# Layer 0's second product as seven block products in a hand-written order, with the weight sums and the transfers around it rearranged

## The chip, the cores and the metric

One core of one Trainium2 chip. The metric is device time in microseconds (us) of one execution. The kernel before takes 1918.76 us, the median of 3 runs (1918.51 to 1919.03). All runs told of here are of the fast state, at a mean granted TensorE clock of 0.995 to 1.00. "Ratio" is always the mean time of one kernel's fast runs over the mean time of the fast runs of the kernel before in the same rounds, with its 95% interval. It is therefore not quite the ratio of the medians quoted beside it.

## The reference, cut to what matters

Four layers run one after the other on x of 128 x 64 x 256 in f32: a graph network, an LSTM over sliding windows, causal attention, and masked attention. Only layer 0's second product, the start of layer 1 and one round of layer 3 are touched.

```python
# layer 0, after the aggregation over neighbours; rows = 8192 (16 chunks of 512)
h   = relu(batchnorm(agg @ W1.T + b1))     # 512 features
out = h @ W2.T + b2                        # 512 -> 256: the product that is changed
out = batchnorm(out)                       # needs mean and variance over all rows
x   = x + out
# layer 1 begins with a graph aggregation; then, for p = 1..4, an LSTM over windows:
g = x_t @ Wih[p].T + h @ Whh[p].T + (bih + bhh)
```

## The kernel before: the parts that count

The second product of one chunk has an output of 256 features x 512 rows, in two blocks of 128 features. Each block sums four matmuls of 512 columns.

```python
def product2(chunks, by_block):
    h1 = {c: l0b.tile([P, KH, CH], F32, tag="h1") for c in chunks}
    banks = {(c, m): bank(f"z2_{c}_{m}") for c in chunks for m in range(KD)}
    for k in range(KH):
        for c in chunks:                                   # batch norm and ReLU, ScalarE
            nc.scalar.activation(h1[c][:, k, :], z1[c][k], AF.Relu, bias=..., scale=...)
    for c, m, k in order:                                  # 8 matmuls of 512 columns
        nc.tensor.matmul(banks[c, m], w2_sb[:, k, m*P:(m+1)*P], h1[c][:, k, :], ...)
    for c in chunks:
        for m in range(KD):                                # VectorE: statistics, then eviction
            nc.vector.bn_stats(st2[:, m, c, :], banks[c, m])
            nc.vector.tensor_scalar(z2[c][:, m, :], banks[c, m], bn2_sb[...], None, op0=OP.add)
```

Beside it GpSimd prepares the LSTM's weights for a seven-product scheme of its own. Twelve gates go, one after the other, through two buffers: load, four sums, store.

```python
def weight_sums(p, q):
    w = stage.tile([P, 16, P], F32, tag="ws", bufs=2)
    nc.sync.dma_start(w[...], wih_t / whh_t)               # two loads
    for dst, a, b, op in (...):                            # four sums on GpSimd
        nc.gpsimd.tensor_tensor(v[:, :, dst], v[:, :, a], v[:, :, b], op)
    nc.sync.dma_start(far[:, :9], w[:, :9])                # two stores
    nc.sync.dma_start(far[:, 9:], w[:, 10:])

for c in range(2, NCH):
    if wanted: weight_sums(*wanted.pop(0))
    product2([c], False)
...
bias = ...; nc.sync.dma_start(bias, bih); nc.sync.dma_start(bias2, bhh)
nc.vector.tensor_add(bias, bias, bias2)                    # the LSTM's bias
...
load_sets(6)                                               # prepared weights, six gates
... early <- x                                             # x of the first chunks
```

## Time and profile before

| What | Before |
|---|---|
| Median time | 1918.76 us |
| Span of the profiled execution | 1916.9 us |
| TensorE busy | 1896.7 us (99%) |
| Second product, all 16 chunks, from its first matmul to the one after it | 143.90 to 255.08 us: 111.18 us |
| One chunk in it | 16 records x 0.429 = 6.87 us |
| GpSimd's last weight sums stored | issued at 216.4 us, 39 us before the end of the stretch |
| x issued, x used | 243.25 us, 261.06 us |

How to read it: TensorE is busy in all but 20 us, so a gain comes from fewer columns streamed through it. The other engines matter only where they hold it up. The lines behind this are shown in the prediction. One more row serves for the comparison later: a stretch of 6.05 us in the middle of the product in the kernel before. Columns: PE, PEld (weight loads), DVE (VectorE), ACT (ScalarE) and POOL (GpSimd) busy, each with its number of instructions, then granted clock, DMA share and GB/s.

```profile
186.80:192.85 6.05, 6.05 (x16) 2.68 (x15) 2.03 (x4) 2.11 (x4) 4.73 (x7) 1.00 0.51 202
```

VectorE and ScalarE are a third busy; GpSimd runs ahead with the weight sums at its own pace.

### The profile page before, as it was taken

What the parts mean: (1) busy time and instruction counts of PE and PEld (TensorE: products, weight loads), DVE (VectorE), ACT (ScalarE), POOL (GpSimd) and SP (SyncE); (2) the same over time, 40 slices, a digit from 0 to 9 for tenths busy, and PEclk for the clock granted to TensorE, in tenths of its full rate; (3) what the DMA queues carried; (4) which work ended last, traced back from release to release, by engine and by line L of the source; (5) the groups of instructions that cost most, each with busy time, mean ns of one, the idle gap of its engine ahead of it and who ended that gap; (6) DMA issues with size and microseconds to landing.
All of it is one profiled execution on the core that took longest, in us unless ns stands there. A gap on an engine that the chain in (4) does not pass through costs nothing.

```text
span 1916.9 us, 38323 instructions
## 1 busy us (share of the span) xinstructions
PE 1896.7 (99%) x14981; PEld 1459.5 (76%) x14981; DVE 1158.1 (60%) x3020; ACT 957.9 (50%) x2132; POOL 414.0 (22%) x615
## 2 busy tenths in 40 slices
PE   9999999999999999999999999999999999999998
PEld 5444465897897889699689789879969967777776
DVE  6644354546557655755755765665555557777776
ACT  5654434445456455455545645545554534444453
POOL 4205210221211121121121121112112113232232
PEclk9999999999999999999999999999999999999999
DMA  4216712224524521532542452253144245444433
GB/s 138 67 32 228 275 49 67 83 83 160 159 83 144 181 100 61 177 105 94 187 143 83 160 182 84 72 196 109 59 160 127 92 128 159 133 143 146 143 111 111
DMA packets 110500, 240.36 MB, mean 125 GB/s; under 512 B 11376, under 2 KB 74352, under 8 KB 110320
## 3 DMA queue, kind: packets, MB, share of 16 engines
q1 hardware_dynamic: 109568, 236.57, 37.1%
q8 instruction: 119, 1.95, 0.4%
q0 software_dynamic: 320, 1.05, 0.2%
q14 instruction: 61, 0.50, 0.1%
q10 hardware_dynamic: 432, 0.30, 0.1%
HBM read 169.98 MB, written 67.90 MB: 124 GB/s over the span
## 4 chain that ended last, share of the span: by engine, by line
PE 94%; DVE 3%; ACT 1%; issue 1%; POOL 1%; DMA 0%; DVEq 0%; SPq 0%; ACTq 0%; POOLq 0%
PE x L848 23%; PE g L812 18%; PE z L848 11%; PE y L848 6%; PE z L377 6%; PE v L1120 6%; PE z L360 5%; PE p_q L1127 3%; PE u L593 3%; PE v L579 3%; PE X L1316 3%; PE Y L1316 1%; PE agg_c L214 1%; PE o L1241 1%; PE agg_b L214 1%; PE o L1443 1%
## 5 line engine op out<-in xcount | busy, mean ns | idle before, releaser
L857 DVE TENSOR_TENSOR gates<-gates,x 128x128 f32<-128x128 f32 (+2 forms) x384 | 119.4, 322 | 335.6 <-PE x L848 333.4
L848 PE MATMUL x<-xd,wset 128*128 128x128 f32 (+2 forms) x1280 | 284.9, 310 | 0.1
L848 PE MATMUL x<-hd,wset 128*128 128x128 f32 (+2 forms) x1152 | 246.7, 303 | 0.0
L848 PEld LDWEIGHTS x<-xd,wset 128*128 128x128 f32 x1280 | 202.1, 190 | 16.9 <-DVE gates L857 3.0
L906 POOL TENSOR_TENSOR gates<-gates 128x512 f32<-128x512 f32 (+2 forms) x48 | 74.8, 1559 | 648.1 <-ACT gates L740 648.1
L740 ACT ACTIVATE gates<-gates,bias 128x256 f32<-128x256 f32 (+4 forms) x384 | 170.4, 491 | 66.4 <-DVE gates L857 63.6
L848 PEld LDWEIGHTS x<-hd,wset 128*128 128x128 f32 x1152 | 185.1, 191 | 5.0
L791 ACT ACTIVATE gates<-g,bias 128x512 f32<-128x512 f32 (+2 forms) x240 | 138.0, 609 | 98.1 <-PE g L812 94.8
L812 PE MATMUL g<-hT,wset 128*128 128x256 f32 (+2 forms) x744 | 184.4, 405 | 1.1 <-DVE hT L751 1.1
L812 PEld LDWEIGHTS g<-hT,wset 128*128 128x128 f32 x744 | 140.5, 190 | 44.1 <-issue 8.9
L812 PE MATMUL g<-hT,wih 128*128 128x512 f32 x384 | 166.4, 592 | 0.0
L854 ACT COPY gates<-y 128x128 f32<-128x128 f32 (+2 forms) x192 | 54.1, 293 | 205.2 <-PE y L848 204.7
L848 PE MATMUL z<-hs,wset 128*128 128x128 f32 (+2 forms) x768 | 154.1, 303 | 0.0
L812 PEld LDWEIGHTS g<-hT,wih 128*128 128x128 f32 x384 | 72.3, 190 | 87.7 <-issue 83.2
L848 PEld LDWEIGHTS z<-hs,wset 128*128 128x128 f32 x768 | 119.8, 191 | 3.3
L360 PE MATMUL z<-agg,w_sb 128*128 128x512 f32 x256 | 114.1, 598 | 0.0
L797 DVE TENSOR_TENSOR cell<-gates 128x512 f32<-128x512 f32 (+2 forms) x80 | 50.5, 648 | 100.3 <-ACT gates L791 100.3
L377 PE MATMUL z<-h,w_sb 128*128 128x512 f32 x256 | 110.2, 592 | 0.0
L857 DVE TENSOR_TENSOR gates<-gates,z 128x128 f32<-128x128 f32 (+2 forms) x384 | 104.6, 316 | 0.1
L854 ACT COPY gates<-x 128x128 f32<-128x128 f32 (+2 forms) x192 | 56.5, 295 | 93.9 <-PE x L848 93.1
L740 ACT ACTIVATE gates<-x,bias 128x128 f32<-128x128 f32 (+2 forms) x192 | 74.7, 389 | 50.9 <-PE x L848 48.1
L848 PE MATMUL z<-hT,wset 128*128 128x128 f32 (+1 forms) x512 | 96.9, 301 | 0.0
(245 smaller groups left out, 3637.1 us busy)
## 6 DMA issues: line engine op xcount, KB each, us to landing
wset<-wfar SPq DMA_DIRECT2D x96, 960.0 KB, 6.4
hT<-far_h SPq DMA_DIRECT2D x124, 128.0 KB, 2.8
far_h<-hm SPq DMA_DIRECT2D x16, 512.0 KB, 4.1
far_n<-xs SPq DMA_DIRECT2D x16, 512.0 KB, 6.6
xs<-far_n SPq DMA_DIRECT2D x64, 128.0 KB, 3.4
far_x<-xs SPq DMA_DIRECT2D x16, 512.0 KB, 3.0
x<-far_x SPq DMA_DIRECT2D x64, 128.0 KB, 3.2
xt<-in_x_dram SPq DMA_DIRECT2D x15, 512.0 KB, 4.0
```

The lines of the kernel that those rows point to most:

```text
L360: nc.tensor.matmul(ps, w1_sb[:, k, m * P : (m + 1) * P], agg[:, k, :], start=(k == 0), stop=(k == KD - 1))
L377: nc.tensor.matmul(banks[c, m], w2_sb[:, k, m * P : (m + 1) * P], h1[c][:, k, :], start=(k == 0), stop=(k == KH - 1))
L579: nc.tensor.matmul(banks[m], wg0_sb[:, k, m * P : (m + 1) * P], agg[:, k, :], start=(k == 0), stop=(k == KD - 1))
L740: nc.scalar.activation(gate(q, c, part), src, AF.Tanh if q == 2 else AF.Sigmoid, bias=bs[:, q * KD + c : q * KD + c + 1])
L791: nc.scalar.activation(columns_of(gate(q, c)), natural(banks[q, c][:, :n].rearrange("p (w b) -> p w b", b=nb)), AF.Tanh if q == 2 else AF. ...
L812: nc.tensor.matmul(banks[q, c][:, :n].rearrange("p (w b) -> p w b", b=nb)[:, w, :], block(q, c, k), hv[:, k, w.start * p : (w.stop - 1) * ...
L848: nc.tensor.matmul(folded(self.psum(kind)), wsets[p, self.q][:, BLOCKS[kind][i], :], (ox[self.s] if part == "x" else oh)[kind], start=firs ...
L854: nc.scalar.copy(gate(self.q, kind // 5, halves[kind // 5]), self.psum(kind))
L857: nc.vector.tensor_add(gate(self.q, *dst), gate(self.q, *a), self.psum(kind))
L906: nc.gpsimd.tensor_mul(gates[:, 0, :, :n], gates[:, 0, :, :n], gates[:, 2, :, :n])
L1120: nc.tensor.matmul(ps[:, i, :], hT[:, k, j, :], w[:, k, first : first + D], start=(k == 0), stop=(k == KD - 1))
L1316: nc.tensor.matmul(st[c, tag][:, i * CH // 2 : (i + 1) * CH // 2].rearrange("p (a n) -> p a n", n=P), w, st[c, "o7"][kind], start=first an ...
```

## The change

The output of a chunk is cut into 2 x 2 blocks (features x rows), and the eight block products become seven by forming sums of the weight's blocks once and four sums of the chunk's blocks each time (the Strassen-Winograd form). This is done for chunks 2 to 14; chunks 0, 1 and 15 stay as they were. The scheduler that the kernel is built with no longer orders VectorE, ScalarE and GpSimd in this part: they are put in order by hand, as TensorE was before. The weight sums now stand behind the chunk's own sum in GpSimd's order. x is transferred ahead of the six weight sets, and one round of layer 3 has an exponential behind a copy instead of ahead of it.

The diff, cut to its core (conditions for the first and last chunks left out; `...` marks what is cut):

```diff
+    def differences(engine, dst, b11, b12, b21, b22, third=None):
+        t1, t2, t3, t4 = dst
+        return [lambda: engine.tensor_tensor(t1, b12, b11, OP.subtract),
+                lambda: ((third or engine).tensor_tensor(t3, b22, b12, OP.subtract),
+                         engine.tensor_tensor(t2, b22, t1, OP.subtract)),
+                lambda: engine.tensor_tensor(t4, b21, t2, OP.subtract)]
...
+        for dst, u, v, op in (...):                       # once: sums of w2's blocks
+            nc.gpsimd.tensor_tensor(w2_sums[:, dst], u, v, op)
...
-        for c in range(2, NCH):
-            if wanted:
-                weight_sums(*wanted.pop(0))
-            product2([c], False)
+        for c in range(2, NCH - 1):                       # a = chunk c, b = c + 1, z = c - 1
+            weights = weight_sums(*wanted.pop(0)) if wanted else None
+            next(weights)                                 # loads
+            a.product(2, "Z")
+            if c == 2:
+                ... a.sums ...; result2(0, m, banks[0, m])
+            b.relu(0)
+            z.product(7, "X");  z.add(1, 1, "X")          # frees bank X for product 4
+            b.relu(1)
+            a.product(1, "X");  a.copy(0, 0, "X")
+            z.stats(0)
+            a.product(5, "Y");  a.copy(1, 1, "Y")
+            b.relu(2)
+            a.add(0, 0, "Z")
+            if c == 2: result2(1, m, banks[1, m])
+            z.product(4, "X");  z.copy(1, 0, "X")
+            b.relu(3);  b.begin();  b.sums[0]()
+            z.stats(1)
+            a.product(6, "X");  a.copy(0, 1, "X")
+            b.sums[1]()
+            next(weights)                                 # GpSimd's four sums, stores
+            a.product(3, "Y");  a.add(0, 1, "Y")
+            b.sums[2]()
+            if c in (3, 4):
+                for m in range(KD): stats2(c - 3, m)      # statistics of chunks 0 and 1
...
-    load_sets(6)                                          # the six weight sets
...
+            if n == 1:                                    # now behind the first use of x
+                load_sets(6)
...
-        for c in range(SUP + 2, NCH - SUP - 1):
+        run(ROUND.replace("exp3-3 q2+0 copyq2+0", "q2+0 copyq2+0 exp3-3"), SUP + 2)
+        for c in range(SUP + 3, NCH - SUP - 1):
             run(ROUND, c)
```

More of the change, by code (lines that the diff above doesn't have):

```diff
@@ L324 @@
     st1 = w0.tile([P, KH, NCH, 6], F32, name="st1")
-    z1, hs, aggs = {}, {}, {}
+    z1, z1whole, h1, hs, aggs = {}, {}, {}, {}, {}
     def load0(c):
@@ L356, in product1 @@
                 aggregate0(1)
-                ln_apply(hs[2], *stats2, "a2")
+                ln_apply(hs[2], *third, "a2")
             ps = bank(f"z1_{c}_{m}")
@@ L363, in product1, with relu2 @@
             nc.vector.bn_stats(st1[:, m, c, :], z1[c][m])
-        z2[c] = lo
+        z2[c], z1whole[c] = lo, (lo, hi)
+    def relu2(c, k):
+        nc.scalar.activation(h1[c][:, k, :], z1[c][k], AF.Relu, bias=sh1[:, k : k + 1],
+                             scale=sc1[:, k : k + 1])
     def product2(chunks, by_block):
-        h1 = {c: l0b.tile([P, KH, CH], F32, tag="h1", name=f"h1_{c}") for c in chunks}
         banks = {(c, m): bank(f"z2_{c}_{m}") for c in chunks for m in range(KD)}
-        for k in range(KH):
-            for c in chunks:
-                nc.scalar.activation(h1[c][:, k, :], z1[c][k], AF.Relu, bias=sh1[:, k : k + 1],
-                                     scale=sc1[:, k : k + 1])
         order = [(c, m, k) for c in chunks for m in range(KD) for k in range(KH)]
@@ L378, in product2, with result2, stats2 @@
                              start=(k == 0), stop=(k == KH - 1))
-        for c in chunks:
-            for m in range(KD):
-                nc.vector.bn_stats(st2[:, m, c, :], banks[c, m])
-                nc.vector.tensor_scalar(z2[c][:, m, :], banks[c, m], bn2_sb[:, 0, m : m + 1], None,
-                                        op0=OP.add)
+        return banks
+    def result2(c, m, ps):
+        nc.vector.tensor_scalar(z2[c][:, m, :], ps, bn2_sb[:, 0, m : m + 1], None, op0=OP.add)
+    def stats2(c, m):
+        nc.vector.bn_stats(st2[:, m, c, :], z2[c][:, m, :])
@@ new lines, in new_h1, with __init__, relu, begin @@
+    def new_h1(c):
+        h1[c] = l0b.tile([P, KH, CH], F32, tag="h1", name=f"h1_{c}")
+    class Seven2:
+        def __init__(self, c):
+            self.c, self.banks = c, {}
+            self.b = {(k, j): a[:, :, halves2[j]] for k, a in enumerate(z1whole[c]) for j in range(2)}
+        def relu(self, *ks):
+            for k in ks:
+                one = slice(k, k + 1)
+                nc.scalar.activation(z1[self.c][k], z1[self.c][k], AF.Relu, bias=sh1[:, one],
+                                     scale=sc1[:, one])
+        def begin(self):
+            b = self.b
+            t = l0b.tile([P, 4, KH // 2, CH // 2], F32, tag="h1", name=f"t2_{self.c}")
+            t = [t[:, i] for i in range(4)]
+            self.sums = differences(nc.vector, t, b[0, 0], b[0, 1], b[1, 0], b[1, 1], nc.gpsimd)
+            self.at = {1: b[0, 0], 2: b[1, 0], 3: b[1, 1], 4: t[3], 5: t[0], 6: t[1], 7: t[2]}
+        def product(self, kind, tag):
+            first = tag not in self.banks
+            if first:
+                self.banks[tag] = bank(f"{tag}2_{self.c}")[:, : CH // 2]
+            for k in range(KH // 2):
+                if kind in (1, 2, 4):
+                    m, i = {1: (0, 0), 2: (0, 1), 4: (1, 1)}[kind]
+                    w = w2_sb[:, i * KH // 2 + k, m * P : (m + 1) * P]
+                else:
+                    w = w2_sums[:, {5: 0, 6: 1, 7: 2, 3: 3}[kind], k, :]
+                right = self.at[kind] if hasattr(self, "at") else self.b[{1: (0, 0), 2: (1, 0)}[kind]]
+                nc.tensor.matmul(self.banks[tag], w, right[:, k, :], start=first and not k, stop=True,
+                                 skip_group_check=True)
+        def part(self, m, j):
+            return z2[self.c][:, m, halves2[j]]
+        def copy(self, m, j, tag):
+            nc.scalar.activation(self.part(m, j), self.banks[tag], AF.Identity,
+                                 bias=bn2_sb[:, 0, m : m + 1])
+        def add(self, m, j, tag):
+            nc.vector.tensor_add(self.part(m, j), self.part(m, j), self.banks[tag])
+        def stats(self, m):
+            nc.vector.bn_stats(st2[:, m, self.c, :], z2[self.c][:, m, :])
@@ L387 @@
+    halves2 = [slice(0, CH // 2), slice(CH // 2, CH)]
     with tc.manual_schedule(engines={mybir.EngineType.PE, mybir.EngineType.DVE,
@@ L426 @@
         xt = load0(2)
-        stats2 = xt, *ln_stats(xt, "a2")
+        third = xt, *ln_stats(xt, "a2")
         product1(0)
@@ L436 @@
         nc.gpsimd.dma_start(w2_sb, w2t.rearrange("(k p) f -> p k f", p=P))
+        w2_sums = l0b.tile([P, 4, KH // 2, P], F32, name="w2_sums", bufs=1)
+        a = w2_sb.rearrange("p (i k) (m f) -> p i m k f", i=2, m=KD)
+        for dst, u, v, op in ((0, a[:, 0, 1], a[:, 1, 1], OP.add),
+                              (1, w2_sums[:, 0], a[:, 0, 0], OP.subtract),
+                              (2, a[:, 0, 0], a[:, 0, 1], OP.subtract),
+                              (3, a[:, 1, 0], w2_sums[:, 1], OP.subtract)):
+            nc.gpsimd.tensor_tensor(w2_sums[:, dst], u, v, op)
         for c in range(1, NCH):
@@ L443 @@
         sc1, sh1 = bn_params(st1, bn1_sb, w0, "bn1", True)
-        product2([0, 1], True)
+        for c in range(2):
+            new_h1(c)
+        for k in range(KH):
+            for c in range(2):
+                relu2(c, k)
+        banks = product2([0, 1], True)
         close_l0()
@@ L461, with weight_transposes @@
         c1 = stage.tile([P, KD, P], F32, name="c1")
-        def weight_transposes():
-            for f in range(3 * KD):
+        def weight_transposes(blocks):
+            for f in blocks:
                 ps = bank(f"wt_{f}")
@@ L498, in weight_sums @@
                     src[p - 1].rearrange("(k p) f -> p k f", p=P)[:, :, q * D : (q + 1) * D])
+            yield
             v = w.rearrange("p (i b) f -> p i b f", i=2)
@@ L506, in weight_sums @@
             wfar[p, q] = far
+            yield
         wanted = [(p, q) for p in range(2, SKIP + 1) for q in GATES]
-        for c in range(2, NCH):
-            if c == NCH - 2:
-                weight_transposes()
-            if wanted:
-                weight_sums(*wanted.pop(0))
-            product2([c], False)
-        sc2, sh2 = bn_params(st2, bn2_sb, const, "bn2", False)
+    tc.no_sync_barrier()
+    with tc.manual_schedule(engines={mybir.EngineType.PE, mybir.EngineType.DVE,
+                                     mybir.EngineType.Activation, mybir.EngineType.Pool}):
+        sevens = {c: Seven2(c) for c in range(2, NCH - 1)}
+        sevens[2].relu(2, 3, 0, 1)
+        for c in range(2, NCH - 1):
+            a, b, z = sevens[c], sevens.get(c + 1), sevens.get(c - 1)
+            weights = weight_sums(*wanted.pop(0)) if wanted else None
+            if weights:
+                next(weights)
+            a.product(2, "Z")
+            if c == 2:
+                a.begin()
+                for f in a.sums:
+                    f()
+                for m in range(KD):
+                    result2(0, m, banks[0, m])
+            if b:
+                b.relu(0)
+            if z:
+                z.product(7, "X")
+                z.add(1, 1, "X")
+            if b:
+                b.relu(1)
+            a.product(1, "X")
+            a.copy(0, 0, "X")
+            if z:
+                z.stats(0)
+            a.product(5, "Y")
+            a.copy(1, 1, "Y")
+            if b:
+                b.relu(2)
+            a.add(0, 0, "Z")
+            if c == 2:
+                for m in range(KD):
+                    result2(1, m, banks[1, m])
+            if z:
+                z.product(4, "X")
+                z.copy(1, 0, "X")
+            if b:
+                b.relu(3)
+                b.begin()
+                b.sums[0]()
+            if z:
+                z.stats(1)
+            a.product(6, "X")
+            a.copy(0, 1, "X")
+            if b:
+                b.sums[1]()
+            else:
+                new_h1(c + 1)
+                for k in range(KH):
+                    relu2(c + 1, k)
+            if weights:
+                next(weights)
+            a.product(3, "Y")
+            a.add(0, 1, "Y")
+            if b:
+                b.sums[2]()
+            if c in (3, 4):
+                for m in range(KD):
+                    stats2(c - 3, m)
+        weight_transposes(range(2))
+        a.product(7, "X")
+        a.add(1, 1, "X")
+        a.stats(0)
+        weight_transposes(range(2, 3 * KD))
+        a.product(4, "X")
+        a.copy(1, 0, "X")
+        a.stats(1)
@@ L516 @@
+    tc.no_sync_barrier()
+    with tc.manual_schedule(engines={mybir.EngineType.PE}):
+        c = NCH - 1
+        banks = product2([c], False)
+        for m in range(KD):
+            result2(c, m, banks[c, m])
+            stats2(c, m)
+        sc2, sh2 = bn_params(st2, bn2_sb, const, "bn2", True)
         c2_ps = weight_products()
@@ L688 @@
     BLOCKS = {1: (0, 8), 2: (2, 9), 3: (7, 14), 4: (3, 10), 5: (4, 11), 6: (5, 12), 7: (6, 13)}
-    def differences(engine, dst, b11, b12, b21, b22):
-        t1, t2, t3, t4 = dst
-        return [lambda: engine.tensor_tensor(t1, b12, b11, OP.subtract),
-                lambda: (engine.tensor_tensor(t3, b22, b12, OP.subtract),
-                         engine.tensor_tensor(t2, b22, t1, OP.subtract)),
-                lambda: engine.tensor_tensor(t4, b21, t2, OP.subtract)]
     def lstm(p, hv, sets, name):
```

## The prediction

> **What bounds the kernel now.** I read the page's first part and its chain, then the groups by shape, then the timeline of the stretch that is rewritten (layer 0's second product, 144 to 255 us), then the busy time by window.
>
> ```profile
> span 1916.9 us, 38323 instructions
> PE 1896.7 (99%) x14981; PEld 1459.5 (76%) x14981; DVE 1158.1 (60%) x3020; ACT 957.9 (50%) x2132; POOL 414.0 (22%) x615
> PE 94%; DVE 3%; ACT 1%; issue 1%; POOL 1%; DMA 0%; DVEq 0%; SPq 0%; ACTq 0%; POOLq 0%
> ```
>
> TensorE is busy for all but 20 us and makes 94% of the chain that ends last. So filling gaps can win at most 20 us in the whole kernel. Anything larger must come from giving TensorE fewer columns to stream.
>
> ```profile
> L377 PE MATMUL z<-h,w_sb 128*128 128x512 f32 x256 | 110.2, 592 | 0.0
> L593 PE MATMUL u<-wg_sb,cv 128*128 128x256 f32 x224 | 50.6, 379 | 0.0
> 199.69 40.50 PE L377 MATMUL z<-h,w_sb 128*128 128x512 f32 x94
> 273.05 3.62 PE L593 MATMUL u<-wg_sb,early 128*128 128x256 f32 x16
> ```
>
> The product to be changed is L377: 110.2 us, no idle time. A matmul's mean (592 ns) includes its drain, so spacing is what counts. 94 records in 40.50 us are (40.50 - 0.59) / 93 = 0.429 us apart at 512 columns; 16 in 3.62 us are (3.62 - 0.38) / 15 = 0.216 us apart at 256 columns. Halving the columns halves the cost: small blocks carry no surcharge here, since the 190 ns weight load still fits under 216 ns.
>
> ```profile
> 150.00:200.00 50.00, 50.00 (x118) 22.14 (x117) 22.88 (x35) 22.80 (x32) 24.88 (x37) 1.00 0.68 242
> 200.00:240.00 40.00, 40.00 (x94) 17.62 (x93) 15.22 (x23) 16.66 (x23) 8.91 (x13) 1.00 0.75 277
> ```
>
> Columns: PE, PEld, DVE, ACT, POOL busy, granted clock, DMA share, GB/s. The stretch is pure TensorE at full clock; VectorE and ScalarE are under half busy, so there is room for the additions that fewer products need. GpSimd and DMA carry an independent job: forming the LSTM's weight sums.
>
> **What the Trainium skill says.** "TensorE: Matmul & The Clock Gate", section Back-to-back issue gap, gives a gap linear in the columns N with a fixed part of only 2.5 ns at full clock. The trace agrees on the shape (0.429 against 0.216 us); its f32 records are longer than the page's figure, and I use the trace's. "SBUF — State Buffer", section Who interferes with whom: a VectorE instruction with two SBUF inputs contends with a GpSimd instruction that reads SBUF, and the later one blocks. The trace agrees:
>
> ```profile
> 142.00 0.16 DVE L299 TENSOR_TENSOR sc_bn<-sc_bn,bn_sb 128x1 f32<-128x1 f32 x1 [1.01 <-POOL sc_bn L100]
> 150.26 5.74 POOL L502 TENSOR_TENSOR ws<-ws 128x256 f32<-128x256 f32 x8
> 150.32 0.67 DVE L299 TENSOR_TENSOR sc_bn<-sc_bn,bn_sb 128x1 f32<-128x1 f32 x1 [0.99 <-POOL sc_bn L100]
> ```
>
> The same one-column VectorE instruction takes 0.16 us with GpSimd idle and 0.67 us while GpSimd runs a sum of 0.72 us. This is my main worry, since the change puts two-input VectorE sums beside GpSimd sums.
>
> **The change part by part.**
> 1. Fewer products. The output of a chunk is 2 x 2 blocks; before, 8 matmuls of 512 columns, each shown as two records: 16 x 0.429 = 6.87 us. After, 7 block products with two matmuls of 256 columns: 28 records x 0.216 = 6.05 us. This is done for chunks 2 to 14; 0, 1 and 15 stay. 13 x 0.82 = 10.6 us off TensorE, all on the path.
> 2. Work added per chunk, against a budget of 6.05 us. ScalarE: 4 normalizations with ReLU of 512 columns at 0.72 to 0.80 us (pairs take 1.50) plus 4 copies out of PSUM of 256 columns at 0.37 us (row of L484): about 4.5 us. VectorE: 3 sums of 512 columns at 0.69 us (L797), 3 additions from PSUM at 0.42 us (L857, 256 columns), 2 statistics at 0.69 us: 4.7 us. GpSimd: one sum of 512 columns, 1.3 to 1.4 us, and the 4 weight sums at 0.72 us: 4.3 us. Each fits, so in steady state TensorE should stay the bound.
> 3. The tight loop on ScalarE. From the end of product 5 to the next chunk's first product come copy, ReLU, copy, ReLU: 0.2 us wake-up, then about 0.3 + 0.7 + 0.3 + 0.8 = 2.3 us. TensorE has three products between, 3 x 0.864 = 2.59 us. Slack 0.3 us.
> 4. Start. VectorE has for chunk 2 its own sums, four evictions of chunks 0 and 1 at 0.73 us and the sums of chunk 3, about 7.6 us, while TensorE has only 5 products, 4.3 us. Part is done ahead under the product of chunks 0 and 1. ScalarE's last ReLU of chunk 3 comes out about 0.4 us late by my hand walk. Cost 0.4 us.
> 5. Statistics of chunks 0 and 1 are pushed into chunks 3 and 4: 2 x 0.69 = 1.4 us more on VectorE there, 6.1 us against 6.05. They stand ahead of an addition that frees bank X for product 4. I count 0.6 us of stall each: 1.2 us.
> 6. Shared port. Three VectorE sums, 3 x 0.62 = 1.9 us, plus GpSimd's 1.3 + 2.9 us make 6.1 us of mutually exclusive time per 6.05 us, if nothing overlaps. It is just saturated, so GpSimd slides slowly and has about 5 us to slide over 12 chunks before its sum is needed by product 7. I count 0.8 us.
> 7. Sums of w2's blocks on GpSimd during the first product: 4 x 0.72 us after w2 lands (about 25 us), so to 28 us. The next GpSimd instruction started at 27.68 us before; up to 0.3 us, counted 0.2.
> 8. The end. Statistics now follow the eviction, but eviction plus statistics took 0.7 + 0.73 us in the other order before, ahead of the same aggregate, and one small addition goes: 0.
> 9. x ahead of the weight sets. Before, x was issued at 243.25 us and used at 261.06, so it was no wait. Afterwards it can issue once chunk 14's blocks are read, about 10 us before the end of the product, and needs 4.5 us. The six weight sets, 7.5 us each, end well before their use about 54 us after that end. 0: it protects against what part 1 shifts.
> 10. Layer 3: one round has an exponential moved behind a copy:
>
> ```profile
> 1614.46 1.20 PE L1210 MATMUL s<-hT,q 128*64 128x64 f32 x32 [0.83 <-ACT q L1188]
> ```
>
> This wait is 0.83 us. The VectorE half of that copy ended at 1613.96 us, so about 0.4 us of it goes.
>
> Sum: -10.6 + 0.4 + 1.2 + 0.8 + 0.2 - 0.4 = -8.4 us; 1918.76 - 8.4 = 1910.4 us, 0.4% less.
>
> **The rivals.**
> A. Everything hides. Then only the columns and layer 3 count: -11.0 us, 1907.8. For it: the two idle halves of VectorE and ScalarE, and that the same seven-product form in layer 3 (L1316) runs with only 0.3 us of idle time on TensorE. Against it: there the sums are all on GpSimd and other work lies between.
> B. The shared port becomes the bound. If the exclusive time is 6.4 us per chunk (0.69 us each for VectorE's sums and 1.44 for GpSimd's), it sets the pace for 12 chunks and about half the gain goes: 12 x 0.35 = 4.2 us lost, 1914. For it: the 0.67 us above. Against it: around 580 us VectorE and GpSimd sums of 128 columns run side by side with GpSimd's at 0.48 to 0.59 instead of 0.45 us, so part of an instruction does overlap.
> C. The weight sums' transfers become the bound.
>
> ```profile
> 162.34 5.75 POOL L502 TENSOR_TENSOR ws<-ws 128x256 f32<-128x256 f32 x8 [6.34 <-DMA ws<-in_whh_t_dram]
> 174.07 5.74 POOL L502 TENSOR_TENSOR ws<-ws 128x256 f32<-128x256 f32 x8 [5.98 <-DMA ws<-in_whh_t_dram]
> ```
>
> Two gates go through per 11.73 us, that is 5.87 us per gate: sums, store, load again in the same two buffers. The new pace is one per 6.05 us, so the loop has 0.2 us of slack per gate. Since GpSimd now also carries a sum that TensorE needs, a late load would hold it. Before, the sums ran ahead freely and ended at 218 us of 255. If the loop takes 6.4 us, 12 x 0.35 = 4 us of delay mostly disappears in the 5 us of room named in step 6: 0 to 2 us, 1911 to 1913.
> D. Something breaks outside, such as late x or late weight sets at the start of the LSTM: some 5 us, 1915. The queue order speaks against it.
>
> **Range and chances.** A gives the lower edge, B plus small stalls the upper: 1906.5 to 1915 us should hold it 8 times in 10, middle 1910. Two per cent would be 38 us; the product touched is only 110 us long, so neither side is credible: faster by over 2% 0.01, within 2% 0.98, slower 0.01.
>
> **What would show each step.** Step 1: about 364 fewer-column records of 256 columns at 0.216 us spacing in place of 208 of 512, and the stretch from chunk 2's first product to chunk 14's last near 79 us. Steps 4 and 5: idle time of TensorE only in the first three chunks, released by ScalarE's ReLU or VectorE's addition. Step 6 or B: VectorE's sums of 512 columns at over 1 us instead of 0.69, and idle time in every chunk up to the twelfth. C: GpSimd's sums idle for a DMA before them, followed by TensorE idle at products 5 or 7. Step 10: the 0.83 us before L1210 halves. I would be wrong if the span fell by less than 4 us (B or D) or by more than 12 us, which would mean that gaps elsewhere closed as well.

## The result, and the profile after

The changed kernel takes 1910.8 us, the median of 6 runs (1910.04 to 1914.43), against 1918.89 us (1918.28 to 1919.99) for the kernel before in the same rounds. The ratio is 0.996 [0.9948, 0.9973]: the same, by the 2% mark, and 8 us less. In a second call the same kernel gave 1911.72 us.

From the page of the changed kernel (span; busy time of each engine; the chain that ended last):

```profile
span 1908.6 us, 38821 instructions
PE 1887.0 (99%) x15137; PEld 1488.3 (78%) x15137; DVE 1190.7 (62%) x3070; ACT 979.5 (51%) x2184; POOL 444.6 (23%) x632
...
PE 93%; DVE 4%; ACT 1%; issue 1%; POOL 1%; DMA 0%; SPq 0%; DVEq 0%; ACTq 0%; POOLq 0%
```

TensorE's busy time fell by 9.7 us, the span by 8.3, and VectorE's part of the chain grew from 3 to 4%. TensorE is still the bound. The same 6.05 us of the stretch as above, now:

```profile
186.80:192.85 6.05, 6.05 (x30) 5.32 (x29) 5.20 (x8) 4.49 (x9) 4.77 (x5) 1.00 0.64 234
```

It now holds a whole chunk, and TensorE is still fully busy. VectorE went from 2.03 to 5.20 us, ScalarE from 2.11 to 4.49: the work moved onto them and stays beside TensorE. TensorE's timeline shows the pace (start, length, instruction):

```profile
186.80 1.03 PE L432 MATMUL X<-t,w_sums 128*128 128x256 f32 x4
...
192.85 1.03 PE L432 MATMUL X<-t,w_sums 128*128 128x256 f32 x4
```

Product 6 of one chunk starts 192.85 - 186.80 = 6.05 us after that of the chunk before, and each product of four records takes 0.86 us.

From its first matmul to the one that follows it, the stretch is 246.78 - 144.37 = 102.41 us, 8.77 us shorter. The columns alone give 13 x (6.87 - 6.05) = 10.7 us. The rest is idle time: I listed every start of a block product that came later than its predecessor's number of records x 0.216 us after it. These gaps sum to 1.93 us, nearly all while chunks 3 to 5 are worked on (163 to 180 us). The two large ones stand before product 4. This is the second of them, with the VectorE and GpSimd lines around it (L311: a sum of two SBUF blocks; L580: weight sums; L393: the statistics of chunk 0; L443: the addition that frees bank X):

```profile
171.01 0.88 DVE L311 TENSOR_TENSOR t<-z1b,t 128x512 f32<-128x512 f32 x1
...
171.43 2.43 POOL L580 TENSOR_TENSOR ws<-ws 128x256 f32<-128x256 f32 x3
...
171.82 1.27 DVE L393 BATCH_NORM_STATS2 st<-z1a 128x6 f32<-128x512 f32 x2
...
173.01 0.40 DVE L443 TENSOR_TENSOR z1a<-z1a,X 128x256 f32<-128x256 f32 x1
...
173.47 1.13 PE L432 MATMUL X<-t,w_sb 128*128 128x256 f32 x4 [0.64 <-DVE z1a L443]
```

The addition is late because two statistics (1.27 us) stand right ahead of it, and because two sums before them took longer beside GpSimd: 0.88 instead of 0.69 us (shown) and, from 169.16 us on, 1.59 instead of 0.69 us. Ahead of the first gap, at 166.51 us, VectorE is late by the two evictions of chunk 1 (from 161.31 us) and by the blocked sum shown next.

The mutual waiting of VectorE and GpSimd is plainly seen where GpSimd's sum comes first (L309: GpSimd's sum of 512 columns, L310: VectorE's):

```profile
162.91 1.54 POOL L309 TENSOR_TENSOR t<-z1b,z1a 128x512 f32<-128x512 f32 x1 [4.44 <-ACT z1b L411]
...
163.41 1.58 DVE L310 TENSOR_TENSOR t<-z1b,t 128x512 f32<-128x512 f32 x1
...
164.92 0.41 DVE L443 TENSOR_TENSOR z1a<-z1a,Y 128x256 f32<-128x256 f32 x1
```

A VectorE sum that takes 0.69 us alone takes 1.58 us here, where it started in the middle of GpSimd's. Where VectorE's sum came first, at 182.17 us, it kept its 0.69 us and GpSimd's took 1.78 us instead of 1.27. The addition with one operand in PSUM (L443) keeps its 0.41 us although GpSimd is running weight sums then. So these instructions behave by the rule that the prediction took from the skill: those with two SBUF inputs contend, and the later one waits.

### The profile page after: what moved, and what is told of

It reads as the page before. It is cut to its first block, busy times and chain, and to the rows that moved or that the text cites. A ratio compares the mean times of both kernels' runs of the same rounds, so it can differ in the third digit from the quotient of the medians.

```text
span 1908.6 us, 38821 instructions
## 1 busy us (share of the span) xinstructions
PE 1887.0 (99%) x15137; PEld 1488.3 (78%) x15137; DVE 1190.7 (62%) x3070; ACT 979.5 (51%) x2184; POOL 444.6 (23%) x632
## 3 DMA queue, kind: packets, MB, share of 16 engines
q0 software_dynamic: 320, 1.05, 0.2%
## 4 chain that ended last, share of the span: by engine, by line
PE 93%; DVE 4%; ACT 1%; issue 1%; POOL 1%; DMA 0%; SPq 0%; DVEq 0%; ACTq 0%; POOLq 0%
PE x L990 23%; PE g L954 18%; PE z L990 11%; PE y L990 6%; PE v L1264 6%; PE z L369 5%; PE p_q L1271 3%; PE u L743 3%; PE v L729 3%; PE X L1460 3%; PE X L432 2%; PE Y L1460 1%; PE z L385 1%; PE Y L432 1%; PE agg_c L214 1%; PE o L1587 1%
## 5 line engine op out<-in xcount | busy, mean ns | idle before, releaser
L369 PEld LDWEIGHTS z<-agg,w_sb 128*128 128x128 f32 x256 | 47.3, 190 | 54.6 <-issue 51.4
```

Source lines behind the costliest of these rows:

```text
L369: nc.tensor.matmul(ps, w1_sb[:, k, m * P : (m + 1) * P], agg[:, k, :], start=(k == 0), stop=(k == KD - 1))
```

## The experiments

Eleven kernels were run; numbers 9 to 11 ran on another chip, where the kernel before took 1919.45 us. "Stretch" is the length defined above (before 111.18, changed 102.41 us); "gaps" is the sum of TensorE's gaps among the block products (changed: 1.93 us).

The granted clock has to be watched behind the stretch. In three of the profiles (statistics spread, evictions on ScalarE, x behind the sets) the clock was granted at one half for 3.41, 3.41 and 13.65 us, from about 259 to 261 us on; in the other ten it is 1.00 there. This is that time in the first of them (columns as above; the third from the end is the granted clock):

```profile
258.94:262.35 3.41, 3.41 (x25) 2.25 (x21) 3.03 (x11) 0.76 (x2) 1.10 (x3) 0.50 1.04 426
```

Six matmuls that only keep TensorE busy take 1.54 us there and 0.87 us in the changed kernel's profile, and the LSTM comes 1.0 us later than TensorE's waits before it explain. What brings it about was not tested: all three profiles have a late load and so a wait of TensorE shortly before, but two others with such a wait (numbers 1 and 4) keep 1.00.

### 1. The changed kernel again

No edit; it is the base of the comparisons.

> The changed kernel itself, beside the next three on the same chip. Expected 1910.8 us as before, 8.1 us under the kernel before it, with TensorE idle 0.34 us and 0.64 us before product 4 in chunks 3 and 4 and 0.17 us in chunk 5.

Measured: 1911.72 us (1909.78 to 1912.89, 5 runs), ratio 0.9957 [0.9944, 0.9971]; stretch 102.52 us, gaps 2.02 us. The stretch repeats within 0.1 us, but the profiled span is 1910.7 us against 1908.6 in the first profile. The difference arises behind the stretch: from the first of the transposes there (L239) to the first matmul of the LSTM it is 28.50 us here and 26.63 in the first profile (and in the kernel before). Here are VectorE and TensorE there in this execution, and then the same addition in the first profile of the changed kernel (L687: the LSTM's bias addition; L239: the transposes, which follow the last statistics):

```profile
246.78 0.19 DVE L687 TENSOR_TENSOR bias<-bias,bias 128x32 f32<-128x32 f32 x1 [2.54 <-DMA bias<-in_bhh_dram]
...
253.93 1.86 PE L239 MATMUL at_b<-ident,cv 128*128 128x128 f32 x15 [1.65 <-DVE cv L714]
```

```profile
244.72 0.19 DVE L687 TENSOR_TENSOR bias<-bias,bias 128x32 f32<-128x32 f32 x1 [0.41 <-DMA bias<-in_bhh_dram]
```

The small addition of the LSTM's two biases stands in VectorE's order between the eviction of chunk 15's first half and its statistics. Its operand was loaded at the start in the kernel before. Now its load is issued at 241.66 us (first profile), behind the weight sums' last store at 238.57. It lands at 244.62 us there, which costs VectorE 0.41 us and the LSTM nothing, and 2 us later, at 246.68, in this execution. Experiment 9 tests this.

### 2 to 4. What makes VectorE late before product 4

Statistics of chunks 0 and 1 spread over chunks 7 to 10, one each:

```diff
-            if c in (3, 4):
-                for m in range(KD):
-                    stats2(c - 3, m)
+            if 7 <= c < 11:
+                stats2((c - 7) // 2, (c - 7) % 2)
```

> The four statistics of chunks 0 and 1 go from chunks 3 and 4 (two each) to chunks 7 to 10 (one each). Theory: two statistics together push VectorE's addition past product 4, one does not. Then the gaps of chunks 4 and 5 go (0.81 + 0.17 us with what follows them) and that of chunk 3 stays, as no late statistics stand before it: about 1.0 us less than the changed kernel. Rival: VectorE, held up at the port it shares with GpSimd, is full in every chunk; then the gaps only move to chunks 7 to 10 and the time stays.

Chunk 1's evictions on ScalarE instead of VectorE:

```diff
             a.product(1, "X")
+            if c == 2:
+                for m in range(KD):
+                    nc.scalar.activation(z2[1][:, m, :], banks[1, m], AF.Identity, bias=...)
             a.copy(0, 0, "X")
...
-            if c == 2:
-                for m in range(KD):
-                    result2(1, m, banks[1, m])
```

> The two evictions of chunk 1 go from VectorE to ScalarE, which sat idle 2.9 us there. Theory: the gap of chunk 3 comes from VectorE being late with chunk 3's sums because of its evictions. Then that gap goes (0.49 us) and those of chunks 4 and 5 shrink somewhat, since VectorE starts 0.5 us or more ahead: 0.5 to 1.0 us less than the changed kernel. Rival: the second sum waits for GpSimd's sum, not for VectorE's turn; then the gap of chunk 3 stays.

Both edits together:

> Both edits. Theory: all gaps of the stretch go, 1.5 us of idle time and 0.4 us of slow restarts: 1909 us, 1.5 to 1.9 us less than the changed kernel. Rival as above: less than 0.5 us.

Measured:

| Kernel | Median (range), us | Ratio | Stretch, us | Gaps, us |
|---|---|---|---|---|
| changed | 1911.72 (1909.78 to 1912.89) | 0.9957 [0.9944, 0.9971] | 102.52 | 2.02 |
| statistics spread | 1911.82 (1911.17 to 1912.79) | 0.9961 [0.9948, 0.9973] | 102.39 | 1.88 |
| evictions on ScalarE | 1913.3 (1910.81 to 1914.44) | 0.9966 [0.9954, 0.9979] | 104.17 | 3.65 |
| both | 1912.37 (1910.26 to 1915.27) | 0.9965 [0.9952, 0.9977] | 104.20 | 3.65 |

None gained: the first expectation's rival came true (the time stays), and the stretch of the second and third kernels is 1.7 us longer where 0.5 to 1.9 us less was expected. Spreading the statistics took the two gaps away where they had been and made two new ones of 0.47 us where they went, again before product 4 and again behind VectorE's addition. This is the first of them:

```profile
195.80 0.68 DVE L393 BATCH_NORM_STATS2 st<-z1a 128x6 f32<-128x512 f32 x1
...
196.85 1.13 PE L432 MATMUL X<-t,w_sb 128*128 128x256 f32 x4 [0.31 <-DVE z1a L443]
```

So the statistics do cause gaps. Two of the four places that they were moved to opened one: VectorE has little to spare in those chunks, too.

The evictions on ScalarE closed the gap of chunk 3, as its theory said, and halved the next one (0.44 us left of 0.81); but they opened new ones from 222 us on, at products 3 and 2, the largest of 1.5 us at the end, at product 3. From the timeline of that kernel (L580: weight sums, L309: GpSimd's chunk sum, L439: ScalarE's copy):

```profile
232.52 2.90 POOL L580 TENSOR_TENSOR ws<-ws 128x256 f32<-128x256 f32 x4 [3.97 <-DMA ws<-in_whh_t_dram]
...
235.38 1.26 POOL L309 TENSOR_TENSOR t<-z1b,z1a 128x512 f32<-128x512 f32 x1
...
236.68 0.47 ACT L439 ACTIVATE z1a<-Y,bn_sb 128x256 f32<-128x256 f32 x1 [2.81 <-POOL t L309]
...
237.20 1.13 PE L432 MATMUL Y<-z1b,w_sums 128*128 128x256 f32 x4 [1.30 <-ACT z1a L439]
```

Read from the top: a weight sum waits 3.97 us for its load; the chunk's own sum stands behind it and starts at 235.38; the copy overwrites a block that this sum still has to read, so it waits for the sum; product 3 needs bank Y, which the copy empties, so TensorE waits for the copy. This is rival C of the prediction, in a variant of the kernel. Two groups of rows tell how near the changed kernel is to the same edge (GpSimd's weight sums in the changed kernel, then with the evictions on ScalarE; the last part is idle time before them and its cause):

```profile
L580 POOL TENSOR_TENSOR ws<-ws 128x256 f32<-128x256 f32 x48 | 40.2, 858 | 4.5 <-DMA ws<-in_whh_t_dram 3.5
```

```profile
L580 POOL TENSOR_TENSOR ws<-ws 128x256 f32<-128x256 f32 x48 | 41.2, 878 | 11.8 <-DMA ws<-in_whh_t_dram 10.8
```

In the changed kernel the time from the landing of a gate's second load to its first sum shrinks from 2.3 us at the third gate to 0.2 us at the eighth, so hardly any reserve is left. Its first wait of over 1 us comes with the last gate's weight sums, at 235.27 us, where no chunk's sum follows. What tipped the loop over with the ScalarE edit can be read from SyncE's order, in that kernel and then in the changed one (L573: loads of a gate; L582, L583: stores of the gate before):

```profile
196.91 0.38 SPq L573 DMA_DIRECT2D ws<-in_wih_t_dram  x1
198.08 0.32 SPq L582 DMA_DIRECT2D wfar<-ws  x1
...
198.91 0.86 SPq L573 DMA_DIRECT2D ws<-in_whh_t_dram  x1
```

```profile
198.37 0.38 SPq L573 DMA_DIRECT2D ws<-in_wih_t_dram  x1
198.80 0.47 SPq L573 DMA_DIRECT2D ws<-in_whh_t_dram  x1
```

In both kernels with the ScalarE edit the seventh gate's second load stands behind the stores of the gate before and is issued 2.0 us after the first load, not 0.43 us; the eleventh gate's is as late (2.3 to 2.5 us). In the changed kernel this happens to the last gate alone (2.6 us), and it holds up the last store, and so what queues behind it. The scheduler still orders SyncE, so an edit on ScalarE may have moved these loads; no run held SyncE's order fixed.

### 5. x behind the weight sets again

```diff
+    load_sets(6)
     hTs = {}
...
-            if n == 1:
-                load_sets(6)
```

> The changed kernel with the six weight sets put back ahead of x in the queue, all else kept. My prediction's step 9 gave the move 0 us. In the changed kernel's trace the sets are issued only at 244.8 us and take 12.9 us each to land, and x is needed at 252.7. New theory: behind 5.9 MB at some 420 GB/s, x lands about 14 us after 244, near 259 us, and TensorE waits 5 to 8 us: 1916 to 1919 us. Rival, step 9 as predicted: no change, 1910.8.

Measured: 1922.63 us (1921.41 to 1923.66), ratio 1.0016 [1.0001, 1.0031]; stretch 102.42 us, the same. From the first transpose to the LSTM it is 39.16 us, instead of 28.50 in number 1 and 26.63 in the first profile. The reason in that kernel's timeline (L773: the first instruction that needs x):

```profile
263.86 0.69 DVE L773 TENSOR_TENSOR xs<-early,at_b 128x512 f32<-128x512 f32 x1 [10.51 <-DMA early<-in_x_dram]
...
268.35 2.40 PE L214 MATMUL agg_b<-adjt_bd,cv 64*64 64x64 f32 x64 [11.33 <-ACT cv L187]
```

And the DMA queue, in the kernel before and in this one (start, length of issuing, transfer):

```profile
216.37 0.43 SPq L505 DMA_DIRECT2D wfar<-ws  x1
...
220.54 11.53 SPq L549 DMA_DIRECT2D wset<-wfar  x6
243.25 0.94 SPq L611 DMA_DIRECT2D early<-in_x_dram  x2
```

```profile
238.10 0.43 SPq L583 DMA_DIRECT2D wfar<-ws  x1
...
243.35 3.88 SPq L701 DMA_DIRECT2D wset<-wfar  x6
247.65 1.95 SPq L762 DMA_DIRECT2D early<-in_x_dram  x2
```

Before, the weight sums ran ahead freely and their last store was out at 216.4 us, so the six weight sets had moved when x was issued (the last landed at 243.46 us). Behind hand-ordered sums the last store is out 22 us later, and everything that queues behind it crowds together at the end of the stretch. With the sets ahead of it, x lands 16 us after its issue, and TensorE waits 11.33 us; the expectation had 5 to 8. About 1 us more is lost after that, where the clock is granted at one half (259.78 to 273.43 us). The move of x is no protection against a small risk: it is worth 11 us here, more than the seven products win. Without it the change would have been no faster than the kernel before (ratio 1.0016, by the 2% mark the same).

### 6. The round of layer 3 alone, in the kernel before

```diff
-        for c in range(SUP + 2, NCH - SUP - 1):
+        run(ROUND.replace("exp3-3 q2+0 copyq2+0", "q2+0 copyq2+0 exp3-3"), SUP + 2)
+        for c in range(SUP + 3, NCH - SUP - 1):
             run(ROUND, c)
```

> The kernel before with the layer 3 edit alone. My prediction gave it 0.4 us. The changed kernel's trace shows the wait of 0.83 us gone, but a new wait of 0.26 us at the transposes and the same distance from the round's start to its sixth matmul group after them. Theory: the softmax chain on VectorE ends at the same time and takes back all of it: 0 us (within 0.2). Rival: 0.4 us faster.

Measured: 1918.96 us (1918.27 to 1919.46), ratio 0.9997 [0.9982, 1.0013]. The wait of 0.83 us that the prediction shows is gone, and nothing is won. TensorE in the changed kernel (L1354 is the matmul that waited):

```profile
1603.52 1.89 PE L1264 MATMUL v<-wvo_sb,hT 128*128 128x256 f32 x8
1605.34 1.61 PE L1354 MATMUL s<-hT,q 128*64 128x64 f32 x32
1606.88 1.99 PE L1264 MATMUL v<-wvo_sb,hT 128*128 128x256 f32 x8
...
1611.78 0.41 PE L1298 MATMUL tr<-ident,s 128*128 128x128 f32 x2 [0.26 <-DVE s L1289]
```

In the kernel before these four start at 1611.74, 1614.46, 1615.59 and 1620.02 us. The changed kernel is 8.22 us ahead at the first, 9.12 at the second (0.90 won), 8.71 at the third, because the group of 32 takes 1.61 instead of 1.20 us, and 8.24 at the fourth, because the transpose now waits 0.26 us for VectorE. All of the 0.90 us comes back within 6.5 us.

### 7. An eighth product that collides

An extra block product 1 into a bank of its own was put behind the copy of product 1:

```diff
+            a.product(1, "W")
             a.product(5, "Y")
```

> The changed kernel with one more block product per chunk into a bank that nobody reads (the result stays right). Theory: TensorE sets the pace in every chunk, so 13 x 0.864 = 11.2 us more, less the gaps of 1.5 us that are then filled: 9.7 to 11.2 us more, 1920.5 to 1922. Rival: VectorE with GpSimd, over 90% busy there, set the pace from time to time and would hide part of it: under 8 us more.

Measured: 1930.6 us (1930.05 to 1931.01), ratio 1.0058 [1.0044, 1.0072]; stretch 123.24 us, 20.8 us longer. The added columns are only 13 x 4 x 0.216 = 11.2 us. The experiment was ill made: the extra product reads the block that the copy just before it overwrites, so it waits for ScalarE, 7.9 us in 13 waits. It says nothing on the pace of a chunk, and was made again as number 11.

### 8. No weight sums on GpSimd

The four weight sums are replaced by clearing their places. The result is wrong on purpose (relative error 0.028); transfers and stores stay.

```diff
-                nc.gpsimd.tensor_tensor(v[:, :, dst], v[:, :, a], v[:, :, b], op)
+            nc.gpsimd.memset(w[:, 4:8], 0.0)
+            nc.gpsimd.memset(w[:, 12:16], 0.0)
```

> The changed kernel with GpSimd's weight sums replaced by fills that read nothing (wrong result on purpose; transfers kept). Theory: VectorE's waits at the shared port come half from the weight sums, half from GpSimd's own third sum. VectorE's first and third sums of a chunk fall from 0.95 and 0.88 to about 0.69 us, its second stays near 1.6; the gaps of chunks 3 to 5 shrink but do not go; time 0.5 to 1.5 us less. Rival: the port costs nothing on TensorE's path; time unchanged within 0.3 us.

Measured: 1909.47 us (1909.27 to 1909.79), ratio 0.9948 [0.9935, 0.9962]; stretch 101.58 us, gaps 1.05 us, and the LSTM 26.63 us after the stretch. Of the 1.9 us of gaps, 0.9 go with GpSimd's weight sums: contention with them is part of the cause. It is not all of the contention: VectorE's first sum of a chunk falls to its undisturbed 0.69 us (0.92 in the changed kernel), as expected, but the third, expected at 0.69, takes 1.32 us beside GpSimd's own chunk sum, which stayed; the second takes 0.83, not 1.6. The spread of the times is 0.5 us, against 3.1 of the changed kernel; the last store goes out at 232.25 us here, so the bias is in time as well.

### 9. The bias loaded early

```diff
         nc.gpsimd.dma_start(bn2_sb, bn2)
+        bias = const.tile([P, SKIP, KG], F32, name="bias")
+        bias2 = const.tile([P, SKIP, KG], F32, name="bias2")
+        nc.sync.dma_start(bias, bih)
+        nc.sync.dma_start(bias2, bhh)
+        nc.vector.tensor_add(bias, bias, bias2)
...
-    (the same five lines behind the product)
```

> The changed kernel with the LSTM's two bias loads and their addition put back to the start of the stretch, ahead of all weight sums. Theory (the executions of the changed kernel that take 1911 to 1914 us are those in which the bias lands late, behind the weight sums in the queue, and holds VectorE's last evictions): the addition of the biases is gone from the end of the stretch, the LSTM starts 26.6 us before its end mark again instead of 28.5, and the time is 1909 to 1910.5 us in every execution, a spread under 1.5 us; ratio 0.9945 to 0.9955. Rival (the spread comes from x or from the weight sums' own transfers): median 1911.5 as before, spread 3 us or more.

Measured: 1910.39 us (1908.71 to 1910.64, 5 runs), ratio 0.9953 [0.994, 0.9965]; stretch 102.41 us, gaps 1.92 us. The bias is added at 25.5 us, and at the end of the stretch VectorE's eviction at 243.44 us is followed by its statistics at 244.22 with no wait between.

Of the changed kernel's 11 executions, 6 took 1911.2 to 1914.43 us; here none of 5 took over 1910.64. The spread is 1.9 us and not under 1.5, because of one execution at 1908.71; the other four lie within 0.4. The LSTM comes 26.63 us after the first transpose again. The long executions are gone, as the theory said. By the ratios alone this kernel and the changed one are not told apart; that rests on the two profiles in number 1 and on the absence of long executions among five.

### 10. The statistics where VectorE has time

The early bias, and the four statistics of chunks 0 and 1 behind the last block product, where VectorE waits for chunk 15's product:

```diff
-            if c in (3, 4):
-                for m in range(KD):
-                    stats2(c - 3, m)
...
         a.stats(1)
+        for c in range(2):
+            for m in range(KD):
+                stats2(c, m)
```

> The early bias, and besides it the four statistics of chunks 0 and 1 moved out of chunks 3 and 4 to behind chunk 14's last statistics, where VectorE waits for the product of chunk 15 (6.9 us, room for four of 0.69 us). Theory (VectorE being late before product 4 is those statistics plus the contention): TensorE's gaps in the stretch fall from 1.9 us to 0.5 to 1.0 us, and the time is about 1 us under that of the early bias alone, 1908 to 1909.5 us. Rival (contention with GpSimd alone makes VectorE late, so the gaps only move, as when the statistics were spread): gaps stay at 1.6 to 2.0 us and the time is that of the early bias alone within 0.3 us.

Measured: 1909.4 us (1908.08 to 1910.11, 5 runs), ratio 0.9948 [0.9936, 0.9961]; stretch 101.34 us, gaps 0.83 us. It is 1.0 us under number 9 by the medians and 1.07 us by the stretch. The four statistics take 2.46 us from 239.84 us on, and the last chunk's first eviction follows them at 242.21, so they hold nothing up. At the place of the second gap, product 4 has no wait any more:

```profile
171.50 0.41 DVE L443 TENSOR_TENSOR z1a<-z1a,X 128x256 f32<-128x256 f32 x1
...
172.35 1.03 PE L432 MATMUL X<-t,w_sb 128*128 128x256 f32 x4
```

This is the best kernel found, about 10 us under the kernel before. The gap of chunk 3 (0.51 us) is still there. Its lead over number 9 is seen in the stretch; the intervals of the ratios overlap.

### 11. An eighth product that collides with nothing

```diff
             a.product(2, "Z")
+            a.product(2, "W")
```

> The changed kernel with one block product more in each of its 13 chunks (product 2 done a second time into a bank of its own that nobody reads), so that it waits for no copy and holds none up. Theory (TensorE sets the pace of every chunk, with no other engine close behind): 13 x 4 x 0.216 = 11.2 us more, less up to 1.5 us for gaps that it fills: 9.7 to 11.2 us over the changed kernel, stretch 112 to 114 us. Rival (VectorE, ScalarE and GpSimd together set the pace at about 6.05 us): the added 0.86 us per chunk lies partly beside their work, and the time grows by less than 8 us.

Measured: 1917.96 us (1917.61 to 1918.98, 4 runs), ratio 0.9995 [0.9979, 1.001]. By the time alone the rival's number was hit: 6.2 us over the changed kernel of the second call and 7.6 over number 9, not 9.7 to 11.2. The trace tells another thing. TensorE is busy for the whole of a chunk that is now 6.91 us long, and the others have the time they had:

```profile
186.00:192.91 6.91, 6.91 (x34) 6.08 (x33) 5.21 (x8) 4.49 (x8) 5.02 (x6) 1.00 0.60 218
```

The stretch is 255.68 - 143.84 = 111.84 us. The added columns are 11.23 us, and the gaps fell from 1.93 to 0.12 us: 102.41 + 11.23 - 1.81 = 111.83. So the added product lies on the path in full, less the gaps that the added time closed. My bound of 1.5 us for these was too low. With 0.86 us more per chunk, GpSimd waits for no load either (0.9 us idle before all 48 weight sums, instead of 4.5).

What is left of the difference lies outside the stretch. Against number 9's profile, TensorE is 9.02 us behind after the stretch, 8.36 at its last group of matmuls, and the span ends 7.2 us later. The first 0.66 us is nearly all one pause, told of in the last section, that is 1.28 us there and 0.64 us here. The rest, 1.2 us, is the last output transfer, which took that much less.

## Why the prediction was right

The time, 1910.4 us, was met: 1910.8 us. By its steps:

- Step 1, fewer products, -10.6 us: right. 28 records x 0.216 us make 6.05 us per chunk, as the timeline shows, and experiment 11 shows that a product added there costs its columns.
- Step 2, the work added fits: right. VectorE was reckoned at 4.7 us and is busy 5.2; ScalarE 4.5 and 4.49; GpSimd 4.3 and 4.77. TensorE is full in a steady chunk.
- Step 3, the loop over ScalarE, with slack of 0.3 us: no gap after the third chunk is put down to it in the changed kernel.
- Step 4, the start, +0.4 us: right in mechanism, too large. The wait for ScalarE's last ReLU of chunk 3 is there, at product 2 (163.21 us), and costs 0.10 us. Then comes the gap of 0.50 us at product 4, which VectorE causes.
- Steps 5 and 6, late statistics 1.2 us and the shared port 0.8 us: right in mechanism and in sum (2.0 against 1.93 us of gaps), but not two separate terms. The statistics' move took 1.09 us away (experiments 9 and 10), the weight sums' removal 0.9 us (experiment 8). Each gap is both together: an addition late by 1.3 or 1.4 us of statistics or evictions and by about 1.1 us of blocked sums (0.90 and 0.19 us ahead of the second gap).
- Step 7, w2's sums, +0.2 us: not seen; the stretch starts 0.47 us later in the first profile, but between 0.06 us earlier and 0.59 later in other kernels that have these sums, which is noise.
- Step 8, the end, 0: this step failed in one of the two profiled executions and, to judge by their times alone, in about half of the 11. I had looked at the order of eviction and statistics and not at what else the scheduler had put between them. The bias addition there waited for a load that is now queued behind the weight sums: up to 1.9 us.
- Step 9, x, 0: right for the kernel as it is, but for a weaker reason than I gave. I said that x is issued 10 us before the end of the product and needs 4.5 us. It is issued 3 us before the end, at 243.83 us, behind the weight sums' last stores and the loads that follow them in SyncE's order, and needs 6.3 to 7.4. It still comes before its use at 252.77. "It protects against what part 1 shifts" was right and undersized: experiment 5 puts it at 11 us.
- Step 10, layer 3, -0.4 us: wrong. The wait goes, and the time comes back within 6.5 us (experiment 6).

The sum, from the profile: -8.77 us in the stretch, +0.47 at its start by noise, 0 at its end in the first profile, 0 in layer 3, so -8.3 us. The prediction's -8.4 had +0.4, +0.2 and -0.4 in it that did not occur (or came as 0.1) and nearly cancel, with 0 in place of a bias wait of 0 to 1.9 us. So part of the closeness is luck. The longest execution, 1914.43 us, is more than a bias wait of 1.9 us explains. It left no trace, and its cause stays open; its mean granted clock, 0.998, is the lowest of its six, so a stretch at half clock as in three of the profiles is a candidate, not shown.

Of the rivals, A (everything hides) is refuted by the gaps. B (the port sets the pace) is refuted by a steady chunk of 6.05 us with TensorE full. C (the transfers) holds up no block product in the changed kernel, but by the eighth gate its reserve is used up, its last gate's sums wait 3.18 us for their load, and experiments 3 and 4 fell over that edge. D, late transfers outside, was what came in some executions, with a small size, through the bias rather than through x.

## What to carry to other kernels

When an engine that ran ahead freely is tied to the order of the bound engine, look at what stands in line behind its last action: here the weight sums' last store moved back by 22 us, and with it every load behind it in that queue. If a scheduler still orders that queue, read its order from the trace after every edit. Issue small loads that need nothing, such as a bias, before such a train, and put the load that is needed first at its head. Additional work for an engine that is 85% busy beside a full TensorE is free only where TensorE is doing something that does not need it; moving it to other busy chunks opened new gaps in two of four (experiment 2).

## What the Trainium skill lacked or had wrong

- "TensorE: Matmul & The Clock Gate", section Back-to-back issue gap, gives the gap for N columns, N / 2.4 + 2.5 ns for a matmul by itself and other figures for a sustained stream, without saying what f32 costs. The f32 stream here follows the first form. The runs show two records of 0.429 us for an f32 matmul of 512 columns, 0.858 us in all, and two of 0.216 us at 256. "FP8 and Floating Point Precision", section TensorE Precision Notes, has the missing factor, four passes: 4 x (512 / 2.4 + 2.5) = 863 ns, an estimate by both pages, which agrees.
- The same page, section LDWEIGHTS (loading the stationary operand), gives 128 / 1.2 = 107 ns for 128 columns and no f32 case; the runs show 190 ns per record.
- "SBUF — State Buffer", section Who interferes with whom, says that the later of the two blocks, but has no size for two sums. The runs show 1.58 instead of 0.69 us for a VectorE sum that came 0.50 us after GpSimd's, and means of 0.92 to 1.21 us over all of VectorE's sums in the stretch, beside GpSimd that is busy about 4.8 of 6.05 us.
- No page that I found tells how long a transfer takes behind others of its queue: x needed 4.5 us in a quiet queue, 6.3 to 7.4 behind the weight loads, and 16 behind six weight sets.
- No page that I found speaks of the pause that the profile puts down to "issue" in the middle of one group of 64 small matmuls near the end: 0.96 us after 50 of them in the kernel before (0.68 in experiment 6), 1.00 to 1.29 us after 20 or 21 of them in the changed one and its variants, and none there but 0.64 us in another group in experiment 11, which has 52 matmuls more. Its place differs between kernels with different numbers of TensorE instructions ahead of it; its cause was not tested, and it makes differences of 1 us between kernels doubtful unless they are read from the stretch concerned.
